# Attention on one core: the projections that run beside the attention steps are cut from pieces of 512 columns into pieces of 256

## The chip, the core and the metric

The kernel is one program on one core of one Trainium2 chip. The core has a matrix engine (TensorE, PE in the profile, with its weight loads listed as PEld), a vector engine (VectorE, DVE), an activation engine (ScalarE, ACT), a general engine (GpSimd, POOL) and a queue that starts most of the DMA transfers (SyncE, SP). Each engine works off its own instruction stream in order; where one needs what another makes, it waits for a semaphore. Matmuls write into PSUM, in banks of 128 partitions by 512 float32 columns.

The metric is the device time of one execution in microseconds (us). Lower is better.

## The reference

A state `x` of 4096 tokens by 256 features passes through four residual layers: attention a, a soft mixture of experts, attention b, and the mixture of experts again with the same weights. Each gets the layer norm of its input.

```python
x = x + attn_a(layernorm(x), Wq, Wk, Wv, Wo, bo, denom_bias)
x = x + ffn(layernorm(x), phi_w, phi_b, expert_w, expert_b)
x = x + attn_b(layernorm(x), q_w, k_w, v_w, o_w)
x = x + ffn(layernorm(x), phi_w, phi_b, expert_w, expert_b)

def attn(x):                     # 16 heads of 16 features, 1 x 4096 x 256
    q, k, v = heads(x @ Wq.T), heads(x @ Wk.T), heads(x @ Wv.T)
    sim = causal(q @ k.T / sqrt(16))
    e = exp(sim - max(sim, -1))
    a = e / (sum(e, -1) + exp(denom_bias))      # the bias in attention a only
    return merge(a @ v) @ Wo.T + bo             # bo in attention a only
```

Everything is float32. In the mixture of experts each token has logits to 64 experts of 32 slots; two softmaxes over them mix tokens into slots and slots back into tokens. Only its edges touch the change.

## The kernel before, in words

**Units and steps.** An attention works in units `(g, b)`: `b` is one of 8 blocks of 512 queries, `g` one of 4 groups of 4 heads. `units` (L339) runs all four groups of block 0, then those of block 1, and so on. A unit has 4(b+1) *steps*, one for each tile of 128 keys up to the diagonal. `steps_b` (L446) yields twice a step: each half makes the scores of two heads in PSUM (`sc`, two matmuls of q and k, L461, and two that subtract the row maxima, `qm`, L466), takes their exponential on ScalarE (L471) and, for a tile on the diagonal, zeroes the upper triangle on GpSimd (`affine_select`, L475). `weigh` (L426) multiplies the exponentials with the values, four heads into one bank `o` (L431); `values_to(1)` keeps it one step behind.

The row maxima must be there before a unit's scores. `steps_a` (L367) makes them ahead, in *pairs*: two matmuls, each into a bank of its own (L380), and two reductions on VectorE (L394, or L388 with the mask where the tile is on the diagonal). How many pairs each step takes is spread evenly by `due` and `wanted` (L551 to L566). `net.bank()` hands out the banks for pairs, projections and transpositions alike, from one pool of three (L329); in the last unit and in the expert layer `net.banks` is a pool of one.

**The order in a step** is written out in the loop at L591 to L616:

```python
want = wanted(n + 1)
maxima_to((done_a[0] + want) // 2)   # about half of the step's pairs
net.beside(2)                        # at most one piece of other work
values_to(1)                         # the o matmuls of the step before
maxima_to(want)                      # the rest of the pairs
```

The prediction calls the first group of pairs A and the last one B. Matmuls and transpositions are kept in the program's order (L67, L70); other instructions may be moved by the scheduler where nothing depends on it.

**Pieces.** `net.beside(k)` (L79) moves a clock on by k, starts what is due on an agenda, and takes one piece from the `urgent` queue, or if that is empty from the `side` queue. `pieces(b)` (L186) lists a block's work for `side`: two normalizations of a token tile (`scale`, on GpSimd at L157, or on ScalarE with `fast`, L152; in attention a the bias is added to `x` at L162), an empty piece, a transposition of two tiles (`turn`, TensorE and a ScalarE copy, L201), an empty piece, the same again for the other two tiles, then two pieces for k and two for q (`part`, L203: 128 output features by the block's 512 tokens, two matmuls accumulating over the 256 input features), and two for v (`values`, L219: two token tiles of 256 features each). That makes 16 pieces. `part` ends in `split` (L165): the projection's leading bits are copied into one half of a buffer by ScalarE (L172), the rest into the other by VectorE (L173), and SP starts the DMAs that lay both out in DRAM (one for k, L175; two for q, L181). There are two such buffers, `hl`, used in turn.

Blocks 0 to 3 of attention a are projected before the first step by `dense` (L234); at `g == 0` of block b = 0 to 3 the loop appends `pieces(b + 4)` (L592). At `g >= 2` of block 3 and later, what is still in `side` is run off before the next unit needs it (L607).

When a unit's values are complete, `epilogue` inverts the sums (6 ticks of the clock later), scales the output (L509, 8 later) and stores it; after the fourth group it fetches the block's output back, and 8 ticks after that two `project` pieces (L530) enter `urgent`: each multiplies two token tiles with `wo` and adds them to `x` (L539). After the second one the block is written to DRAM.

**Attention b's first blocks** are prepared in the expert layer between the attentions. Its last loop goes over 32 token tiles t; from t = 7 it runs one piece a tile, between two halves of the tile's matmuls (L1113). At t = 6 and t = 10 it appends `pieces(0)` and `pieces(1)` with `fast=True` and `values=False`, 14 pieces each (L1126); what is left after the last tile runs off at L1130. The values of these blocks are then made at the start of attention b by `dense_values` (L261).

Of the kernel before, what the change touches and what calls it, by code (L numbers as in the profile page):

```python
# [19 lines left out]
P = 128  # L20
S = 4096
D = 256
NT = S // P
QB = 512
NQB = S // QB
H = 16
HD = 16
# [15 lines left out]
class _Net:  # L43
# [22 lines left out]
    def mm(self, *a, **k):  # L66
        self.tc.keep_in_program_order(self.nc.tensor.matmul(*a, **k))  # L67
# [38 lines left out]
class _Attention:  # L106
# [55 lines left out]
            nc.gpsimd.tensor_tensor(x[:, t, :], x[:, t, :], self.bot, ALU.add)  # L162
        return y

    def split(self, ps, cc, dst, key, part=None):  # L165
        nc = self.net.nc
        two = part is not None
        if not two:
            part = self.hl[self.nhl % 2]
            self.nhl += 1  # L170
        hi, lo = part[:, 0, :], part[:, 1, :]
        nc.scalar.copy(hi.bitcast(F32R), ps)  # L172
        nc.vector.tensor_tensor(lo.bitcast(F32R), ps, hi, ALU.subtract)  # L173
        if key:
            nc.sync.dma_start(  # L175
                dst[ts(cc, 8)].bitcast(F32).rearrange("h e r l t -> (h e) r (l t)"),
                part.rearrange("p l t -> p (l t)").unsqueeze(1).to_broadcast([P, 2, 2 * QB]),
            )
            return
        for r in range(2):  # L180
            (nc.scalar if two and r else nc.sync).dma_start(  # L181
                dst[ts(cc, 8), :, :, r].bitcast(F32).rearrange("h e l t -> (h e) l t"), part
            )


    def pieces(self, b, fast=False, values=True):  # L186
        net, nc = self.net, self.net.nc
        xb, ys = self.xb[b % 2], {}
        idle = lambda: None

        def scale(i):
            if i == 0:
                self.begin(b)
            ys[i] = self.norm(4 * b + i, fast)

        def turn(t2):
            ps = net.bank().rearrange("p (c i t) -> p c i t", c=2, i=2)
            for i in range(2):
                for c in range(2):
                    net.tr(ps[:, c, i, :], ys[2 * t2 + i][:, ts(c, P)])  # L200
            nc.scalar.copy(xb[:, :, ts(t2, 2 * P)], ps.rearrange("p c i t -> p c (i t)"))  # L201

        def part(w, cc, key):  # L203
            ps = net.bank()
            for c in range(2):
                net.mm(ps, w[:, c, ts(cc, P)], xb[:, c, :], start=c == 0, stop=c == 1)
            self.split(ps, cc, (self.kd if key else self.qd)[b], key)

        out = []
        for t2 in range(2):  # L210
            out += [lambda i=i: scale(i) for i in (2 * t2, 2 * t2 + 1)]
            out += [idle, lambda t2=t2: turn(t2), idle]
        for w, key in ((self.wk, True), (self.wq, False)):
            out += [lambda a=(w, cc, key): part(*a) for cc in range(2)]
        if values:
            out += self.dense_values(b)
        return out

    def values(self, b, t2, ps):  # L219
        net, xb = self.net, self.xb[b % 2]  # L220
        ps = ps.rearrange("p (i d) -> p i d", i=2)
        for i in range(2):
            for c in range(2):
                net.mm(
                    ps[:, i, :], xb[:, c, ts(2 * t2 + i, P)], self.wv[:, c, :],
                    start=c == 0, stop=c == 1,
                )
        net.nc.scalar.copy(
            self.vah[:, ds(4 * b + 2 * t2, 2), :, 0:HD],
            ps.rearrange("p i (h e) -> p i h e", e=HD),  # L230
        )
# [32 lines left out]
    def run(self, ready, experts):  # L264

        net, tc, nc = self.net, self.net.tc, self.net.nc
        x, mm = net.x, net.mm
        bo, db = self.bo, self.db
        self.xd = net.xd = net.xds.pop(0)
        with ExitStack() as ctx:  # L270
            pool = lambda n, b, **k: ctx.enter_context(tc.tile_pool(name=f"at_{n}", bufs=b, **k))
            cp = pool("c", 1)
            wo = self.wo
# [10 lines left out]
                out=maskw, in_=maskw, compare_op=ALU.is_ge, fill=NEG,  # L284
# [11 lines left out]
            for p in range(2):  # L296
                f = net.ep.tile([P, QB], F32, name="ot", bufs=3)[:, 0:P]
                nc.gpsimd.memset(f, 0.0)
                for h2 in range(2):
                    for l in range(2):  # L300
                        nc.gpsimd.affine_select(
                            out=f, in_=f, compare_op=ALU.not_equal, fill=1.0,
# [182 lines left out]
            def epilogue(u, ot):  # L485
                g, b = units[u]
                if g == 0:
                    self.ad[b] = net.dram.tile([2 * P, QB], F32, name=f"{self.name}o{b}")
                d16 = net.ep.tile([P, 16], F32, name="d16", bufs=3)
                dd = net.dram.tile([P, 16], F32, name="dd", bufs=3)  # L490
                nc.sync.dma_start(d16, ot[HD:P:32, :].rearrange("j (c s) -> j c s", s=16))
                rb = {}

                def invert():
                    if db is not None:
                        nc.vector.tensor_scalar(d16, d16, edb[:, g : g + 1], None, ALU.add)
                    nc.vector.reciprocal(d16, d16)
                    rb[0] = net.ep.tile([P, QB], F32, name="rb")
                    nc.sync.dma_start(dd, d16)
                    nc.sync.dma_start(  # L500
                        rb[0],
                        dd.rearrange("(j c) s -> j (c s)", j=HG).unsqueeze(1)
                        .to_broadcast([HG, 32, QB]),
                    )
                    net.after(8, divide)

                def divide():
                    on = rb[0]
                    nc.gpsimd.tensor_tensor(on, ot, on, ALU.mult)  # L509
                    for j in range(HG):  # L510
                        nc.sync.dma_start(
                            self.ad[b][ds((HG * g + j) * HD, HD), :], on[ds(32 * j, HD), :]
                        )
                    if g == NG - 1:
                        net.after(4, fetch)

                back = {}

                def fetch():
                    for i2 in range(2):  # L520
                        ao = net.ep.tile([P, 2, 2 * P], F32, name="ao", bufs=2)
                        nc.sync.dma_start(
                            ao, self.ad[b].rearrange("(c p) t -> p c t", p=P)[:, :, ts(i2, 2 * P)]
                        )
                        back[i2] = ao
                    net.after(
                        8, lambda: net.urgent.extend([lambda: project(0), lambda: project(1)])
                    )

                def project(i2):  # L530
                    ps = net.bank().rearrange("p (i d) -> p i d", i=2)
                    for i in range(2):
                        for c in range(2):
                            mm(
                                ps[:, i, :], back[i2][:, c, ts(i, P)], wo[:, c, :],
                                start=c == 0, stop=c == 1,
                            )
                    xs = x[:, ds(4 * b + 2 * i2, 2), :]
                    nc.vector.tensor_tensor(xs, ps, xs, ALU.add)  # L539
                    if i2:  # L540
                        nc.sync.dma_start(self.xd[:, ts(b, 4), :], x[:, ts(b, 4), :])

                net.after(6, invert)
# [46 lines left out]
            n = 0  # L590
# [634 lines left out]
```

## Time and profile before

| | us |
|---|---|
| median of 3 runs | 5162.35 (5161.54 to 5167.37) |
| the profiled execution | 5168.77 |
| its span, first to last instruction | 5167.0 |

The profiled execution has a mean granted TensorE clock of 0.989 of full speed. The span by stage, with the busy time of the engines in it (windows of the trace; a stage ends where the next one's steps begin):

| stage | from, to | length | PE | DVE | ACT | POOL |
|---|---|---|---|---|---|---|
| front | 0, 86.7 | 86.7 | 61.3 | 40.9 | 33.4 | 28.0 |
| attention a, steps | 86.7, 1787.5 | 1700.8 | 1651.4 | 1411.7 | 1101.0 | 172.9 |
| experts, first | 1787.5, 2670.8 | 883.3 | 841.1 | 664.3 | 213.8 | 402.9 |
| attention b, steps | 2670.8, 4367.0 | 1696.2 | 1651.4 | 1405.6 | 1100.7 | 162.8 |
| experts, second | 4367.0, 5167.0 | 800.0 | 780.3 | 624.2 | 181.7 | 391.6 |

Busy time on TensorE comes from modelled ends of pipelined matmuls, so a high share says only that the engine has always something in flight. A float32 matmul appears as two records, of the same shape. In the rows below, a group of instructions shows its source line, engine, operation, output tile and input tiles, shapes and count, then busy time and the mean of one in nanoseconds, then the idle time of the engine just before and what ended it. A timeline's line shows the start, the length in us, the engine, the line, the tiles, how many records it folds together, and in brackets the idle time before it and its cause. Times are counted from the start of the span. L67 is the helper through which every matmul goes, so groups of matmuls are told apart by their tiles.

The pieces that the change touches, by shape, all of them in the span:

| what | line | count | mean ns |
|---|---|---|---|
| k and q parts beside the steps, ScalarE copy 128x512 | L172 | 40 | 583 |
| the same, VectorE subtraction | L173 | 40 | 691 |
| output projections, VectorE addition 128x512 | L539 | 32 | 689 |
| values, ScalarE copy 128x512 (16 of them by `dense_values`) | L228 | 32 | 589 |

### The profile page before, as it was taken

The page shows a single profiled execution, that of the slowest core. Times are in us where ns is not written, and L with a number is a line of the kernel's source. Part 1 is how long each engine was busy: PE and PEld are TensorE (multiplying, and loading weights), DVE is VectorE, ACT ScalarE, POOL GpSimd, SP SyncE. Part 2 cuts the span into 40 slices and gives each one's busy share as a digit, 9 for nine tenths or more (in the row PEclk, how much of TensorE's full clock was granted, in tenths as well). Part 3 has the DMA queues.
Part 4 walks back from the last instruction along what each step waited for, and adds up shares of the span by engine and source line. Part 5 has one row for each costly group of instructions (what it writes and reads, how often), then busy time and mean ns, then how long its engine had stood idle before and what let it go on. Part 6 is the DMA issues. An engine that isn't in the chain of part 4 may idle for free.

```text
span 5167.0 us, 79440 instructions
## 1 busy us (share of the span) xinstructions
PE 4985.5 (96%) x29936; PEld 2669.9 (52%) x29936; DVE 4146.6 (80%) x7800; ACT 2630.7 (51%) x3112; POOL 1158.2 (22%) x1088
## 2 busy tenths in 40 slices
PE   7899999999999999999989999999999999999899
PEld 4444454444455444448854444544444554444588
DVE  5678989898989378777756789888989893887786
ACT  3466676666667721223224666666666677211222
POOL 3211000000000155544411110000000001555453
PEclk9999999999999999999999999999999999999999
DMA  6433222221121013443454342222212210134443
GB/s 254 143 108 125 66 76 65 65 68 58 61 65 56 28 76 106 146 143 120 144 181 143 108 128 68 70 65 69 65 58 64 62 56 32 76 104 149 135 150 110
DMA packets 266449, 499.17 MB, mean 97 GB/s; under 512 B 44976, under 2 KB 110000, under 8 KB 258384
## 3 DMA queue, kind: packets, MB, share of 16 engines
q1 hardware_dynamic: 260832, 485.57, 28.6%
q10 hardware_dynamic: 4896, 7.87, 0.5%
q8 instruction: 235, 3.85, 0.3%
q14 instruction: 150, 1.23, 0.1%
q0 software_dynamic: 336, 0.66, 0.0%
HBM read 336.73 MB, written 156.76 MB: 96 GB/s over the span
## 4 chain that ended last, share of the span: by engine, by line
PE 72%; DVE 13%; POOL 5%; issue 3%; ACT 3%; DMA 2%; SPq 0%; DVEq 0%; POOLq 0%; ACTq 0%
PE o L67 26%; PE bank L67 21%; PE sc L67 16%; DVE mx L394 5%; PE acc L67 4%; PE lg L67 3%; DVE junk L388 3%; POOL e L690 2%; POOL e L698 2%; PE ps L70 2%; ACT e L691 1%; DVE l L677 1%; ACT pb L471 1%; DMA zone<-ld 1%; DMA rb<-dd 0%
## 5 line engine op out<-in xcount | busy, mean ns | idle before, releaser
L471 ACT ACTIVATE pb<-sc 128x1024 f32<-128x1024 f32 (+3 forms) x2304 | 2070.7, 951 | 1132.5 <-PE sc L67 1131.0
L394 DVE TENSOR_REDUCE mx<-bank 128x1 f32<-128x512 f32 x3584 | 2223.0, 682 | 157.5 <-PE bank L67 151.7
L67 PE MATMUL bank<-k,q 64*128 64x512 f32 (+3 forms) x4608 | 1333.9, 451 | 65.0 <-DVE mx L394 26.8
L67 PEld LDWEIGHTS bank<-k,q 64*128 64x128 f32 x4608 | 664.7, 185 | 1177.1 <-DVE mx L394 767.7
L67 PE MATMUL o<-pb,va 128*32 128x512 f32 (+3 forms) x9216 | 1159.7, 574 | 9.1 <-POOL pb L475 7.3
L67 PE MATMUL sc<-q,k 64*128 64x512 f32 (+3 forms) x4608 | 982.5, 389 | 11.3 <-ACT pb L471 10.9
L67 PE MATMUL sc<-qm,one 64*128 64x512 f32 (+3 forms) x4608 | 945.2, 376 | 0.0
L388 DVE CUSTOM_DVE_ANT_0 junk<-bank,maskw 128x128 bf16<-128x128 f32 (+3 forms) x1024 | 502.6, 491 | 253.5 <-PE bank L67 145.8
L475 POOL TENSOR_SCALAR_AFFINE_SELECT pb<-pb 128x256 f32<-128x256 f32 x512 | 205.0, 407 | 2170.0 <-ACT pb L471 2162.7
L67 PEld LDWEIGHTS sc<-q,k 64*128 64x128 f32 x4608 | 507.7, 187 | 129.7 <-issue 50.6
L67 PEld LDWEIGHTS sc<-qm,one 64*128 64x128 f32 x4608 | 524.1, 187 | 68.5
L67 PE MATMUL acc<-e,x 128*128 128x512 f32 x1008 | 464.4, 604 | 22.4 <-POOL e L698 17.8
L691 ACT ACTIVATE e<-e 128x1024 f32<-128x1024 f32 x126 | 133.1, 1057 | 690.2 <-POOL e L690 690.2
L67 PE MATMUL lg<-zone,xnT 128*128 128x512 f32 x1008 | 455.4, 593 | 8.3 <-DVE l L677 7.1
L67 PE MATMUL o<-ys,lT 128*128 128x256 f32 x2048 | 459.5, 381 | 0.0
L67 PEld LDWEIGHTS o<-ys,lT 128*128 128x128 f32 x2048 | 385.6, 191 | 56.5 <-issue 6.6
L67 PEld LDWEIGHTS o<-pb,va 128*32 128x32 f32 x9216 | 183.6, 108 | 319.6 <-issue 286.3
L889 POOL TENSOR_TENSOR e<-l,mc 128x1024 f32<-128x1024 f32 x120 | 281.4, 2365 | 283.3 <-DMA l<-ld 180.5
L67 PEld LDWEIGHTS acc<-e,x 128*128 128x128 f32 x1008 | 189.2, 192 | 264.3 <-issue 211.4
L698 POOL TENSOR_TENSOR e<-e,s 128x1024 f32<-128x1024 f32 x126 | 240.9, 1912 | 366.5 <-DVE s L697 345.0
L67 PEld LDWEIGHTS lg<-zone,xnT 128*128 128x128 f32 x1008 | 189.3, 190 | 245.0 <-issue 213.9
L696 DVE TENSOR_REDUCE s<-e 128x32 f32<-128x1024 f32 x126 | 153.6, 1219 | 158.3 <-ACT e L691 158.1
(136 smaller groups left out, 3229.7 us busy)
## 6 DMA issues: line engine op xcount, KB each, us to landing
k<-ak SPq DMA_DIRECT2D x144, 512.0 KB
k<-bk SPq DMA_DIRECT2D x144, 512.0 KB
ld<-l SPq DMA_DIRECT2D x126, 512.0 KB
l<-ld SPq DMA_DIRECT2D x60, 1024.0 KB
w<-in_L_ffn_expert_w_dram SPq DMA_DIRECT2D x26, 1024.0 KB
q<-aq SPq DMA_DIRECT2D x32, 512.0 KB
rb<-dd SPq DMA_DIRECT2D x64, 256.0 KB
q<-bq SPq DMA_DIRECT2D x32, 512.0 KB
```

The costliest lines, as they stand in the source:

```text
L67: self.tc.keep_in_program_order(self.nc.tensor.matmul(*a, **k))
L70: self.tc.keep_in_program_order(self.nc.tensor.transpose(o, i, self.ident))
L388: nc.vector.tensor_tensor_reduce(out=junk[:, 0:w], in0=scs[h2][:, 0:w], in1=maskw[:, QB - w : QB], scale=1.0, scalar=-3e38, op0=ALU.add, o ...
L394: nc.vector.tensor_reduce(m, scs[h2], AX.X, ALU.max)
L471: nc.scalar.activation(pb[:, :, off:QB], sc[:, :, off:QB], AF.Exp)
L475: nc.gpsimd.affine_select(out=d, in_=d, compare_op=ALU.is_ge, fill=0.0, base=0, pattern=[[0, 2], [1, P]], channel_multiplier=-1,)
L677: net.nc.vector.tensor_tensor(l, lg, self.phb[:, ds(h * (E // 2) + n * 512, 512)], ALU.add)
L690: nc.gpsimd.tensor_tensor(e3, l3, _bc(m.unsqueeze(2), [P, ne, SLOT]), ALU.subtract)
L691: nc.scalar.activation(e, e, AF.Exp)
L696: nc.vector.tensor_reduce(s, e3, AX.X, ALU.add)
L698: nc.gpsimd.tensor_tensor(e3, e3, _bc(s.unsqueeze(2), [P, ne, SLOT]), ALU.mult)
L889: nc.gpsimd.tensor_tensor(e[:, ns, :], l, _bc(cms[t].unsqueeze(1), [P, NH, SLOT]), ALU.subtract)
```

## The change

Each k, q, v and output projection that runs as a piece is cut in two, and each half is a piece of its own, so it is taken in a step (or token tile) of its own. The dense front of attention a and `dense_values` stay as they are.

- `part` takes a half `n`: two matmuls of 256 columns into half a bank.
- `split` works on the half's columns of the same `hl` buffer, moves to the other buffer with each first half, and starts its DMAs after the second half alone.
- The values of `pieces` come from a new method `value`, one token tile at a time.
- `project` works on one token tile; four of them enter `urgent`, and the DMA to DRAM follows the fourth.

A list of `pieces` so grows from 16 to 22 (14 to 18 without values).

```diff
-    def split(self, ps, cc, dst, key, part=None):
+    def split(self, ps, cc, dst, key, part=None, n=None):
         nc = self.net.nc
         two = part is not None
         if not two:
+            self.nhl += n == 0
             part = self.hl[self.nhl % 2]
-            self.nhl += 1
-        hi, lo = part[:, 0, :], part[:, 1, :]
+        cut = part if n is None else part[:, :, ts(n, QB // 2)]
+        hi, lo = cut[:, 0, :], cut[:, 1, :]
         nc.scalar.copy(hi.bitcast(F32R), ps)
         nc.vector.tensor_tensor(lo.bitcast(F32R), ps, hi, ALU.subtract)
+        if n == 0:
+            return
         if key:
...
-        def part(w, cc, key):
-            ps = net.bank()
+        def part(w, cc, key, n):
+            ps = net.bank()[:, 0 : QB // 2]
             for c in range(2):
-                net.mm(ps, w[:, c, ts(cc, P)], xb[:, c, :], start=c == 0, stop=c == 1)
-            self.split(ps, cc, (self.kd if key else self.qd)[b], key)
+                net.mm(
+                    ps, w[:, c, ts(cc, P)], xb[:, c, ts(n, QB // 2)],
+                    start=c == 0, stop=c == 1,
+                )
+            self.split(ps, cc, (self.kd if key else self.qd)[b], key, n=n)
...
         for w, key in ((self.wk, True), (self.wq, False)):
-            out += [lambda a=(w, cc, key): part(*a) for cc in range(2)]
+            out += [lambda a=(w, cc, key, n): part(*a) for cc in range(2) for n in range(2)]
         if values:
-            out += self.dense_values(b)
+            out += [lambda t=t: self.value(b, t) for t in range(4)]
         return out
+
+    def value(self, b, t):
+        net, xb = self.net, self.xb[b % 2]
+        ps = net.bank()[:, 0:D]
+        for c in range(2):
+            net.mm(ps, xb[:, c, ts(t, P)], self.wv[:, c, :], start=c == 0, stop=c == 1)
+        net.nc.scalar.copy(
+            self.vah[:, 4 * b + t, :, 0:HD], ps.rearrange("p (h e) -> p h e", e=HD)
+        )
...
-                        8, lambda: net.urgent.extend([lambda: project(0), lambda: project(1)])
+                        8, lambda: net.urgent.extend([lambda i=i: project(i) for i in range(4)])
...
-                def project(i2):
-                    ps = net.bank().rearrange("p (i d) -> p i d", i=2)
-                    for i in range(2):
-                        for c in range(2):
-                            mm(
-                                ps[:, i, :], back[i2][:, c, ts(i, P)], wo[:, c, :],
-                                start=c == 0, stop=c == 1,
-                            )
-                    xs = x[:, ds(4 * b + 2 * i2, 2), :]
+                def project(i):
+                    ps = net.bank()[:, 0:D]
+                    for c in range(2):
+                        mm(
+                            ps, back[i // 2][:, c, ts(i % 2, P)], wo[:, c, :],
+                            start=c == 0, stop=c == 1,
+                        )
+                    xs = x[:, 4 * b + i, :]
                     nc.vector.tensor_tensor(xs, ps, xs, ALU.add)
-                    if i2:
+                    if i == 3:
                         nc.sync.dma_start(self.xd[:, ts(b, 4), :], x[:, ts(b, 4), :])
```

## The prediction

> **What bounds the kernel now.** I read the page's busy row and its chain first, then the timelines of one bare step and one step that carries a piece, then the groups by shape.
>
> ```profile
> PE 4985.5 (96%) x29936; PEld 2669.9 (52%) x29936; DVE 4146.6 (80%) x7800; ACT 2630.7 (51%) x3112; POOL 1158.2 (22%) x1088
> PE 72%; DVE 13%; POOL 5%; issue 3%; ACT 3%; DMA 2%; SPq 0%; DVEq 0%; POOLq 0%; ACTq 0%
> PE o L67 26%; PE bank L67 21%; PE sc L67 16%; DVE mx L394 5%; PE acc L67 4%; PE lg L67 3%; DVE junk L388 3%; POOL e L690 2%; POOL e L698 2%; PE ps L70 2%; ACT e L691 1%; DVE l L677 1%; ACT pb L471 1%; DMA zone<-ld 1%; DMA rb<-dd 0%
> ```
>
> Busy PE alone proves little, but the chain also runs 72% over PE. The stage to be changed shows why. These are TensorE's timeline (start, length, tile) and VectorE's, around one projection in attention a, query block b=4:
>
> ```profile
> 896.77 0.50 PE L67 MATMUL bank<-k,q 64*128 64x512 f32 x2
> ...
> 898.03 0.52 PE L67 MATMUL bank<-k,q 64*128 64x512 f32 x2
> 898.48 1.06 PE L67 MATMUL o<-pb,va 128*32 128x512 f32 x8
> 899.48 0.50 PE L67 MATMUL bank<-k,q 64*128 64x512 f32 x2
> ...
> 900.74 0.51 PE L67 MATMUL bank<-k,q 64*128 64x512 f32 x2
> 901.36 1.99 PE L67 MATMUL bank<-zone,ao 128*128 128x256 f32 x8
> 903.28 1.06 PE L67 MATMUL o<-pb,va 128*32 128x512 f32 x8
> 904.28 0.50 PE L67 MATMUL bank<-k,q 64*128 64x512 f32 x2
> ```
>
> ```profile
> 900.01 2.48 DVE L394 TENSOR_REDUCE mx<-bank 128x1 f32<-128x512 f32 x4 [0.22 <-PE bank L67]
> 903.46 0.69 DVE L539 TENSOR_TENSOR x<-bank,x 128x512 f32<-128x512 f32 x1 [0.96 <-PE bank L67]
> ```
>
> The bare step, 896.77 to 899.48, takes 2.71 us: eight score matmuls, a maxima pair A, the eight o matmuls, a maxima pair B, without a hole. The step with the piece, 899.48 to 904.28, takes 4.80, and VectorE waits 0.96 us for TensorE in it. So a step with a piece is TensorE's: a piece pays its matmuls, plus the seams at its two ends.
>
> **What a piece costs, and what half a piece will.** A project, k/q or value piece is 1.72 us of matmuls (8 records of 256 columns start every 0.2155, or 4 of 512 every 0.429). The projection step is 4.80 - 2.71 = 2.09 longer, so the seams are 2.09 - 1.72 = 0.37. They can be seen: from A to the piece is 0.62 us (900.74 to 901.36) against 0.45 from A to o in the bare step, as the piece takes the third bank, which waits for the reduction of B before it (+0.17); its first two starts lie 0.32 apart in place of 0.2155 (+0.10); from its last start, 902.97, to o are 0.31 (+0.09). None of the three shrinks with columns. A k piece agrees: the step at 466.98 takes 4.78. So half a piece is 0.86 + 0.36 = 1.22, and two are 2.44 in place of 2.08: **each added piece costs 0.36**. The copy and subtraction end under the o matmuls as now.
>
> **How many are added.** Groups by shape, as engine, shape, count | busy, mean ns | idle:
>
> ```profile
> L172 ACT CAST zone<-bank 128x512 fp32r<-128x512 f32 x40 | 23.3, 583 | 65.2 <-PE bank L67 63.4 <-issue 1.9
> L173 DVE TENSOR_TENSOR zone<-bank,zone 128x512 fp32r<-128x512 f32 x40 | 27.6, 691 | 44.5 <-ACT zone L172 42.9 <-DMA q<-bq 0.6 <-DMA bk<-zone 0.3
> L964 DVE TENSOR_TENSOR x<-o,xl 128x256 f32<-128x256 f32 x64 | 27.2, 424 | 114.3 <-PE o L67 113.9
> ```
>
> 40 k/q parts become 80, the 32 projections (L539) 64, and 16 of the 32 value pieces become 32: 88 more. Taking one piece a step off the queue as beside() does puts 76 of them in attention steps (38 in each attention: 14 in b=0-1, 8 each in b=2 and b=3, 8 in b=4-7), 8 in the first expert part's weighing of tokens and its drain, 4 (the last block's projections) in expert steps.
>
> Two rules of the Trainium skill bear here. The row is a 512-column subtraction of 691 ns against 424 for 128x256 (L964), so two halves take 848, +157. "VectorE: DVE Perf Modes", section "The TRN2 errata", says that each instruction pays a fixed bubble and to tile at 512 elements or more; it speaks against this change. By that rule, with VectorE as the bound, 72 split evacuations x 0.157 = 11 us. By the timeline VectorE stands idle for 0.96 in such a step, so I take 0 for this, and charge the seams. "TensorE: Matmul & The Clock Gate", section "Wait — 56ns, not 53.3ns?", gives a matmul a fixed 2.5 ns; the 160 more records of the 40 split parts would then cost 0.4 us, and the change nothing. The row's starts, 0.2155 for 2 x 256 columns, agree inside a run of matmuls, but the rule has no seam, and 76 x 0.36 = 27.4 us is what the seams make. I take the row: **+27.4**, from 76 x 0.20 = 15 (if the bank wait vanishes) to 76 x 0.50 = 38 (if a bank comes free late as well, an estimate with another 0.14).
>
> **Shifts.** (1) Block 4's pieces no longer fit in the 16 steps of b=0; 6 slip into b=1, and block 5's k, q and values go from b=1 g=0-2 to g=2-3. That moves a GpSimd stall, seen on its timeline:
>
> ```profile
> 177.86 1.29 POOL L509 TENSOR_TENSOR rb<-ot,rb 128x512 f32<-128x512 f32 x1 [14.19 <-DMA k<-ak]
> 179.13 2.42 POOL L157 TENSOR_SCALAR zone<-x,mv,rstd 128x256 f32<-128x256 f32 x2
> 181.52 1.40 POOL L162 TENSOR_TENSOR x<-x,bot 128x256 f32<-128x256 f32 x2
> 182.87 1.48 POOL L475 TENSOR_SCALAR_AFFINE_SELECT pb<-pb 128x256 f32<-128x256 f32 x4
> ```
>
> The diagonal's select stands in GpSimd's queue behind the scaling of block 5, which runs as soon as turn 5 frees its buffer; o waits 4.0 us for it, and the step takes 8.30 (5.68 in attention b) against 2.59 before it. Afterwards turn 5 comes in g=1, two steps ahead of the diagonal, and the stall should go: between 0 and 5.7 + 3.1 = 8.8 us. I take **-6**, as scaling may meet another select. What is late next there is VectorE, with six reductions a step.
>
> (2) The six-reduction steps that receive block 5's halves (3.6-4.0 us) hide little: TensorE waits about 0.42 in them, before the last matmul of B (the record at 249.60 of TensorE's timeline), and the half stands ahead of that, between A and o. I charge it in full.
>
> (3) After each block's last projection ScalarE loads two tables (2 x 1.28) and normalizes x for the expert part. q and v pieces hid under that at b=1-3; fewer matmuls stand there now: 0 to 6 us, I take **+3**, half.
>
> (4) The drain. In the weighing stage one piece runs a token tile, tiles 7 to 31: 25 turns for 28 pieces before, 36 after. What is left runs alone, with one bank:
>
> ```profile
> 2610.61 1.88 PE L67 MATMUL bank<-zone 128*128 128x512 f32 x4
> 2613.90 1.98 PE L67 MATMUL bank<-zone 128*128 128x512 f32 x4 [1.40 <-DVE zone L173]
> 2617.32 3.71 PE L67 MATMUL bank<-zone 128*128 128x512 f32 x12 [1.45 <-DVE zone L173]
> ```
>
> Each 512 part is a chain of matmul, copy, subtraction, 3.43 us; three of them end, with the next piece starting at 2619.36, after 8.75. Afterwards a transposition (4 x 0.11, 0.16 of tail, the 0.59 copy, 0.1: 1.3) and 8 halves are left. A half is 3.43 - 0.86 (matmuls) - 0.2 (copy; 0.38 by L471's 128x256 row) - 0.27 (subtraction) = 2.1; seven of them, the last 2.04 - 0.86 = 1.2, and the 1.3 make 17.2. The weighing loses a transposition and a part, 0.44 + 1.72 = 2.2, which it paid in full (the part at 2605.44 has no seam). Net 17.2 - 8.75 - 2.2 = **+6.2**; 4 to 10.
>
> The split shares its buffer and issues its DMAs once, after the second half, so SP's queue holds no more issues; between a buffer's DMA and its next writing lie two half steps (7.8 us) in place of one (4.8): no wait. The four late projections cost about 0.1 each in expert steps: +0.4.
>
> **Sum.** 27.4 - 6 + 3 + 6.2 + 0.4 = **+31 us**. It is made against the profiled execution, 5168.77 (its span 5167.0 and 1.8 around it), which lies 6.4 over the median of the runs, 5162.35. On the median: **5193**, +0.6%. About 0.2% (10 us) is what a measurement of this kernel tells from no change.
>
> **Rivals.**
> - *Seams vanish* (13%): half pieces fit into waits (PE waits 3.9 us on VectorE's L388 in 161-283) and cost matmuls only. Then -6 + 3 + 6.2 = +3: 5165. For it: early steps of 3-6 us. Against: no hole in the steps of b=3-7.
> - *Relief, faster* (9%): halves fit where TensorE waits for a bank anyway. Block 5's 12 halves in g=2-3 of b=1 then cost nothing and give back 6 x 2.08 = 12.5 an attention, 25 in all; the seams of the other 64 lose their bank wait (x 0.20 = 12.8); the GpSimd stall goes whole (-8.8), the tables cost nothing, drain and late projections 6.6: -14, 5148. It decides if TensorE's wait after B in a six-reduction step is over 0.86 us, the half's matmuls; I read 0.42.
> - *Late banks* (15%): evacuations come late for the next A; 0.6 a piece, 46 us, drain 10, stall stays, tables 6: +62, 5224.
> - *The order of unpinned work shifts* (a table load or scaling lands badly): within the range.
>
> The base case has 63%, with 5172 to 5216 from its low ends (15 - 8.8 + 0 + 4 = +10) and high ends (38 + 0 + 6 + 10 = +54). Range 5164 to 5216, to take in the vanished seams. Faster 0.09; same 0.14; slower 0.77.
>
> **What would show it.** Half steps of 3.9 us in b=3 with 4 records of 256 columns and 0.6 us from A to them; projection steps at b=4-7 four, of about 3.9; no 8.30 step at b=1; a drain of some 17 us before the value pieces of attention b; 80 casts of about 380 ns at L172. I am wrong if half steps take 3.6 or less, or if six-reduction steps stay at 4.0 with a half in them.

## The result, and the profile after

The changed kernel takes 5182.72 us in the median of 7 runs (5177.10 to 5185.74) against 5163.63 for the kernel before beside it (5161.54 to 5175.49, 7 runs). The ratio is 1.0031, 95% interval 1.0021 to 1.0042: slower by 16 us, between 11 and 22. The forecast was 31 us slower, twice as much.

The profiled execution took 5185.74 us, its span 5183.8, at a mean clock of 0.987 (0.989 before). Its page, the busy row and the chain:

```profile
PE 5001.4 (96%) x30096; PEld 2699.2 (52%) x30096; DVE 4167.1 (80%) x7872; ACT 2638.8 (51%) x3168; POOL 1158.3 (22%) x1088
PE 75%; DVE 13%; POOL 4%; issue 3%; ACT 3%; DMA 2%; DVEq 0%; SPq 0%; POOLq 0%; ACTq 0%
```

There are 160 more matmul records than before and the chain runs a little more over TensorE; that tells nothing of where 17 us went. The starts of the steps do. The table sets two pairs of traces of the two kernels (the first traces, and one more of each taken later) against the prediction's own terms, in us:

| stretch | predicted | first pair | second pair |
|---|---|---|---|
| blocks 0 and 1, both attentions | 28 x 0.36 - 6 = +4 | -4.1 | -0.2 |
| blocks 2 and 3 | 32 x 0.36 = +11.6 | +8.0 | +7.0 |
| blocks 4 to 7 | 16 x 0.36 = +5.8 | -6.0 | -4.2 |
| ScalarE's tables, over all blocks | +3 | (in the rows above) | |
| from attention a's last step to attention b's first | -2.2 + 8.45 + 0.4 = +6.6 | +17.9 | +15.9 |
| front and second experts | 0 | +1.0 | -0.8 |
| sum | +31 | +16.8 | +17.7 |

So the attention steps, 60 of whose 76 added pieces lie in blocks 0 to 3, cost almost nothing together (-2.1 and +2.6), and the expert layer that ends in the drain holds the whole loss. The half steps themselves came out as forecast. A block's output projection is now four pieces of one token tile, called quarter projections below; each is half of an old piece. TensorE's timeline of the changed kernel, around two of them in block 5's steps:

```profile
902.32 0.52 PE L67 MATMUL bank<-k,q 64*128 64x512 f32 x2
902.94 1.13 PE L67 MATMUL bank<-zone,ao 128*128 128x256 f32 x4
904.00 1.07 PE L67 MATMUL o<-pb,va 128*32 128x512 f32 x8
904.99 0.50 PE L67 MATMUL bank<-k,q 64*128 64x512 f32 x2
...
906.26 0.51 PE L67 MATMUL bank<-k,q 64*128 64x512 f32 x2
906.87 1.13 PE L67 MATMUL bank<-zone,ao 128*128 128x256 f32 x4
```

From one piece to the next are 3.93 us (902.94 to 906.87); 0.62 lie between A and the piece, as they do with a whole one. 3.93 - 2.70, the bare step, is 1.23 for half a piece; the prediction had 1.22. The smaller evacuations (the copies were forecast at about 380 ns), in the groups by shape (count | busy, mean ns | idle):

```profile
L174 DVE TENSOR_TENSOR zone<-bank,zone 128x256 fp32r<-128x256 f32 x80 | 33.8, 423 | 45.3 <-ACT zone L173 45.3
L173 ACT CAST zone<-bank 128x256 fp32r<-128x256 f32 x80 | 29.7, 372 | 43.6 <-PE bank L67 42.1
```

What paid for the seams is seen after each block's last projection. ScalarE's timeline there, first of the kernel before (projections of block 5):

```profile
1184.82 1.94 ACT L471 ACTIVATE pb<-sc 128x1024 f32<-128x1024 f32 x2 [2.89 <-PE sc L67]
1186.78 1.28 ACT L99 ACT_TABLE_LOAD   x1
1188.07 0.30 ACT L99 ACTIVATE rstd<-mv,eps 128x4 f32<-128x4 f32 x1
1188.39 1.28 ACT L471 ACT_TABLE_LOAD   x1
1189.68 1.94 ACT L471 ACTIVATE pb<-sc 128x1024 f32<-128x1024 f32 x2
```

and of the changed kernel:

```profile
1187.16 1.94 ACT L487 ACTIVATE pb<-sc 128x1024 f32<-128x1024 f32 x2 [1.99 <-PE sc L67]
1189.12 1.28 ACT L99 ACT_TABLE_LOAD   x1
1190.41 0.30 ACT L99 ACTIVATE rstd<-mv,eps 128x4 f32<-128x4 f32 x1
1191.09 1.28 ACT L487 ACT_TABLE_LOAD   x1 [0.38 <-PE sc L67]
1192.38 1.94 ACT L487 ACTIVATE pb<-sc 128x1024 f32<-128x1024 f32 x2
```

VectorE's timeline up to the variances, before (both tiles together) and changed (the last tile):

```profile
1182.93 0.69 DVE L539 TENSOR_TENSOR x<-bank,x 128x512 f32<-128x512 f32 x1 [0.83 <-PE bank L67]
1183.66 0.75 DVE L94 BATCH_NORM_STATS2 st<-x 128x6 f32<-128x256 f32 x2
1184.33 1.27 DVE L394 TENSOR_REDUCE mx<-bank 128x1 f32<-128x512 f32 x2
1185.52 0.24 DVE L95 BATCH_NORM_AGGREGATE mv<-st 128x2 f32<-128x6 f32 x2
```

```profile
1189.21 0.42 DVE L554 TENSOR_TENSOR x<-bank,x 128x256 f32<-128x256 f32 x1
1189.67 0.43 DVE L94 BATCH_NORM_STATS2 st<-x 128x6 f32<-128x256 f32 x1
1190.14 0.18 DVE L95 BATCH_NORM_AGGREGATE mv<-st 128x2 f32<-128x6 f32 x1
```

and TensorE's next wait for ScalarE, before and changed:

```profile
1190.76 0.50 PE L67 MATMUL sc<-q,k 64*128 64x512 f32 x2 [0.82 <-ACT pb L471]
1193.46 0.50 PE L67 MATMUL sc<-q,k 64*128 64x512 f32 x2 [0.17 <-ACT pb L487]
```

Before, the step with the last projection has its exponentials done at 1181.9 and ScalarE idles for 2.89 us while TensorE works at the piece; the loads come only after the next step's exponentials, in a bare step that leaves no such hole, and TensorE then waits 0.82 us for ScalarE. In the changed kernel the loads stand in the last piece's own step, right behind its exponentials (1189.12, while the quarter's matmuls end at 1189.1), and TensorE waits 0.17.

The drain before attention b, TensorE's timeline of the changed kernel:

```profile
2613.67 0.60 PE L70 MATMUL bank<-ident,zone 128*128 128x128 f32 x4
2614.95 1.13 PE L67 MATMUL bank<-zone 128*128 128x256 f32 x4 [0.68 <-ACT zone L204]
2617.29 1.13 PE L67 MATMUL bank<-zone 128*128 128x256 f32 x4 [1.22 <-DVE zone L174]
2619.37 1.13 PE L67 MATMUL bank<-zone 128*128 128x256 f32 x4 [0.95 <-DVE zone L174]
2621.42 1.65 PE L67 MATMUL bank<-zone 128*128 128x256 f32 x4 [0.92 <-DVE zone L174]
2623.99 2.07 PE L67 MATMUL bank<-zone 128*128 128x256 f32 x4 [0.92 <-DVE zone L174]
2627.03 2.08 PE L67 MATMUL bank<-zone 128*128 128x256 f32 x4 [0.96 <-DVE zone L174]
```

and windows over it (stretch, its length, busy time of the five engines, then the granted clock, the DMA share and GB/s):

```profile
2620.00:2630.00 10.00, 6.30 (x15) 3.27 (x13) 1.70 (x4) 1.49 (x4) 0.00 (x0) 0.59 0.87 311
2640.00:2650.00 10.00, 7.91 (x39) 5.17 (x37) 2.96 (x15) 4.42 (x8) 0.00 (x0) 1.00 1.01 367
```

The first halves follow each other every 2.05 to 2.08 us, the chain of matmul, copy and subtraction that the prediction had at 2.1. From 2621 on the same four records take 2.07 in place of 1.13 and the chain 3.0: the clock is at a half. From the transposition to the first value piece, at 2634.89, it is 21.2 us (23.1 in the second trace), where 17.2 were forecast and the kernel before took 8.75 at full clock.

The additions of the token tiles (`x<-o,xl` on VectorE, L964 before, L979 in the changed kernel) divide this stage's excess. Up to the 17th tile, which runs ahead of the first k piece, the changed kernel takes 5.6 and 2.8 us more than before, in the first and the second pair. From there to the 32nd and last it takes 142.2 in both, against 144.3: the -2.2 of the forecast. From that to TensorE's next maxima pair, behind the first value piece, it takes 24.6 and 25.4, against 10.2: +14.4 and +15.3. The first of the three is not the cost of half pieces: a kernel with whole pieces in this layer, shown below, has 2.7 of it in one trace and 0.3 in another.

### The profile page after: what moved, and what is told of

Its sections match the earlier page's. It is cut to its first block, busy times and chain, and to the rows that moved or that the text cites. A ratio compares the mean times of both kernels' runs of the same rounds, so it can differ in the third digit from the quotient of the medians.

```text
span 5183.8 us, 79909 instructions
## 1 busy us (share of the span) xinstructions
PE 5001.4 (96%) x30096; PEld 2699.2 (52%) x30096; DVE 4167.1 (80%) x7872; ACT 2638.8 (51%) x3168; POOL 1158.3 (22%) x1088
## 4 chain that ended last, share of the span: by engine, by line
PE 75%; DVE 13%; POOL 4%; issue 3%; ACT 3%; DMA 2%; DVEq 0%; SPq 0%; POOLq 0%; ACTq 0%
PE o L67 27%; PE bank L67 21%; PE sc L67 16%; DVE mx L410 6%; PE acc L67 5%; PE lg L67 4%; DVE junk L404 3%; POOL e L705 2%; PE ps L70 2%; POOL e L713 1%; ACT e L706 1%; ACT pb L487 1%; DVE l L692 1%; DVE lT L962 0%; DMA d<-ot 0%
## 5 line engine op out<-in xcount | busy, mean ns | idle before, releaser
L67 PE MATMUL bank<-k,q 64*128 64x512 f32 (+3 forms) x4608 | 1320.5, 451 | 65.0 <-DVE mx L410 30.1
```

## The experiments

Each run stands beside the kernel before on the same chip. "Blocks 4 to 7" is the time of their steps in one attention, 1150.4 and 1150.3 us in the first trace of before (attention a and b), 1149.2 and 1150.0 in the second. The times of runs of one kernel spread by 10 to 20 us; in the traces, part of that is where the clock stands at a half in blocks 0 and 1 of an attention (190 us each). Blocks 4 to 7 repeat to about a microsecond, so theories are told apart there.

**The parts apart.** First the projections alone:

```diff
-  net.urgent.extend([lambda: project(0), lambda: project(1)])
+  net.urgent.extend([lambda i=i: project(i) for i in range(4)])
   # with the changed kernel's project; k, q and values as before
```

> Only the output projections are split: four project pieces of one token tile a block in place of two; k, q and values as before. 28 pieces more stand in the attention steps, 4 in expert steps. Theory (each piece more costs its seams, 0.36, but the fourth projection falls under the load of ScalarE's tables, which stalled TensorE after the last projection, and so that stall shrinks by 0.7 to 2.7 a block): 28 x 0.36 = +10, +1 in expert steps, -14 x 1.2 = -17: some -6 us on before, between -12 and 0. Rival (only the seams change, the table stall stays): +11 us. Rival (seams cost nothing in a step that VectorE or ScalarE holds): 0 to +1 for the pieces and -17 for the stall: -16 us.

Measured: ratio 0.9991 (0.9983 to 1.0000), -5 us, as the theory had it, though hardly clear of no change. Blocks 4 to 7 take 1147.8 and 1148.1. Their eight added pieces, at 0.36, would add 2.9; they come out 2.6 and 2.2 lower, so some 5 us an attention went.

Then k, q and values alone, `project` as before:

> The complement: k, q and values in halves as in the changed kernel, the output projections in two pieces as before. Theory: 48 pieces more in the attention steps, 48 x 0.36 = +17, less the GpSimd stall of block 1 (-6), plus the drain before attention b (+14 with the half clock in it): +25 us, between +18 and +30. If the effects of the two parts add, it is the measured +16 to +19 less what the projections alone give. Rival (half pieces of k, q and v cost nothing beside the steps): +8 us.

Measured: 1.0059 (1.0046 to 1.0071), +30 us, at the upper end. The stage before attention b is 14.7 us longer than before (897.9 against 883.2), the attention steps 4.2 and 5.5. The sum of the two parts is +26, against +16 for both together; with intervals of 4 to 7 us to either side, that may be scatter.

**Is the table load the stall?** The square root of the variances by Newton steps on VectorE:

```diff
-  nc.scalar.activation(r, self.mv[:, lo:hi, 1], AF.Sqrt, bias=self.eps)
+  v = self.mv[:, lo:hi, 1]
+  h = self.shift[:, lo:hi]
+  nc.vector.tensor_scalar(r, v, 1.0, 0.5, ALU.add, ALU.mult)
   nc.vector.reciprocal(r, r)
+  for _ in range(4):
+      nc.vector.scalar_tensor_tensor(h, r, -0.5, r, ALU.mult, ALU.mult)
+      nc.vector.tensor_tensor(h, h, v, ALU.mult)
+      nc.vector.scalar_tensor_tensor(r, h, 1.5, r, ALU.add, ALU.mult)
```

> The kernel before, but the reciprocal root of the variances is made by four Newton steps on VectorE in place of ScalarE's square root, so that no table is loaded between the exponentials of an attention. Theory (the tables' load stalls TensorE by 1.8 us after each block's last projection, up to 3 in the early blocks): 14 blocks x 1.8 to 3, less about 0.5 of VectorE in each: -20 us, between -35 and -10. Rival (the stall is ScalarE's normalization of x or is caught up in the following steps): 0, or some us slower for the added VectorE work.

A miss: 1.0027 (1.0016 to 1.0038), 14 us slower, and blocks 4 to 7 at 1150.7 and 1150.9, no better. VectorE's timeline shows why this run doesn't answer the question:

```profile
1196.51 0.16 DVE L104 SCALAR_TENSOR_TENSOR shift<-rstd 128x4 f32<-128x4 f32 x1
1196.70 0.16 DVE L105 TENSOR_TENSOR shift<-shift,mv 128x4 f32<-128x4 f32 x1
1196.90 0.16 DVE L106 SCALAR_TENSOR_TENSOR rstd<-shift,rstd 128x4 f32<-128x4 f32 x1
```

Four columns cost 0.19 us from start to start, so twelve such instructions take 2.3 us of an engine that has 0.2 us of idle time in a bare step, and TensorE then waits for a reduction (0.33 us at 1198.11). One stall was traded for another. Most of the 14 us lie elsewhere: the stage before attention b, where roots are taken too, is 11.6 us longer. A cleaner test leaves the root out and adds nothing:

```diff
-  nc.scalar.activation(r, self.mv[:, lo:hi, 1], AF.Sqrt, bias=self.eps)
+  nc.scalar.activation(r, self.mv[:, lo:hi, 1], AF.Identity, bias=self.eps)
```

> The kernel before with the square root of the variances left out (ScalarE adds the constant and takes no root, so it loads no other table between the exponentials); everything else is issued as before. Theory (the two table loads after a block's last projection stall TensorE by some 1.8 us): the steps of blocks 4 to 7 take 1.8 x 4 = 7 us less in each attention, 1143 in place of 1150. Rival (ScalarE's normalization of x sets that stall, or it is caught up): 1149 or more.

> The projections in four pieces and nothing else split, and the square root left out as in the run beside it. Theory (the split gains only by putting the fourth projection under the table loads): without them it loses its seams, 2 x 0.36 a block, 4 blocks: blocks 4 to 7 take 2.9 us more in each attention than in the run beside it with two projection pieces. Rival (the gain comes from elsewhere, as from statistics made a tile at a time): still 2 us or more less than it.

Each of these two kernels ran once, and its trace is what is read here. Without the root, blocks 4 to 7 take 1144.7 and 1144.3: 5.7 and 6.0 less than with the loads, 1.4 to 1.5 a block. ScalarE's timeline has the hole closed:

```profile
1182.17 1.94 ACT L471 ACTIVATE pb<-sc 128x1024 f32<-128x1024 f32 x2 [2.88 <-PE sc L67]
1184.00 0.30 ACT L99 ACTIVATE rstd<-mv,eps 128x4 f32<-128x4 f32 x1
1184.91 1.94 ACT L471 ACTIVATE pb<-sc 128x1024 f32<-128x1024 f32 x2 [0.61 <-PE sc L67]
```

With quarter projections and no root they take 1147.2 and 1146.5: 2.5 and 2.2 more than with the old two pieces and no root, where eight seams at 0.36 make 2.9. With the root, the same split gained 2.6 and 2.2. So the seams are still paid, to within the microsecond that such sums repeat to, and the gain hangs on the table loads: of the 5.7 to 6.0 us that they cost in four blocks, the split leaves 0.6 and 1.6 (1147.8 - 1147.2, 1148.1 - 1146.5).

**Is it the place or the size that costs?** The halves of the changed kernel, two to a piece, so at the steps of the kernel before:

```diff
-  out += [lambda a=(w, cc, key, n): part(*a) for cc in range(2) for n in range(2)]
+  out += [lambda a=(w, cc, key): [part(*a, n) for n in range(2)] for cc in range(2)]
   # the values and the projections likewise, two token tiles to a piece
```

> The halves of the changed kernel, but two of them taken in one step as one piece: the same small matmuls, copies, additions and the same number of them, at the steps of the kernel before. Theory (an added piece pays 0.36 for its own place between A and o, and not for being half as wide): in a clean step two halves cost 2.09 to 2.3 and not 2.46, so the attention steps come out within 5 us of before, and only the drain is left: +12 us, between +5 and +16. Rival (small instructions pay by themselves, VectorE's 0.157 a pair and the fixed costs of more matmuls): in a clean step 2.46 or more, and the kernel at +20 us or above.

For the steps the theory holds. TensorE's timeline of that kernel, projections of block 5:

```profile
1177.74 0.51 PE L67 MATMUL bank<-k,q 64*128 64x512 f32 x2
1178.35 1.99 PE L67 MATMUL bank<-zone,ao 128*128 128x256 f32 x8
1180.27 1.06 PE L67 MATMUL o<-pb,va 128*32 128x512 f32 x8
```

Eight records follow the same 0.61 us after A as one piece of two tiles did, and the step takes 4.79 (4.82 before in the same step); a k step takes 4.78, as before. Two small copies and subtractions in place of one large pair cost nothing there. Blocks 4 to 7 even fall to 1146.0 in both attentions, since the added tiles' statistics come sooner here too and no place was added. The total was misjudged: 1.0041 (1.0026 to 1.0056), +21 us. The stage before attention b is 24.6 us longer. There the pieces share one bank, and the second half of each pair waits 0.92 us for the first one's subtraction, in the middle of a token tile as well: by the additions of the token tiles, 12.1 us come between the 17th and the last, 7.7 in the drain and behind it, and 4.8 ahead of the first k piece.

**The drain.** The changed kernel with whole pieces in the expert layer, in two separate sets of runs:

```diff
+  if fast:
+      out += [lambda a=(w, cc, key): whole(*a) for cc in range(2)]   # 512 columns
+  else:
       out += [lambda a=(w, cc, key, n): part(*a) for cc in range(2) for n in range(2)]
```

> The changed kernel, but the pieces of attention b's first two blocks, which run in the first expert layer, are whole again (512 columns, 14 a block). Theory (the loss of the change sits in the drain at the end of the expert layer: eight chains of matmul, copy, subtraction in place of two and a bit, and a half clock that comes with them): about 14 us less than the changed kernel, so +2 us on before, within -3 to +6; the row of the granted clock shows no half clock between the last token tile and attention b. Rival (the seams in the attention steps are the loss, and the drain is within the scatter): it stays at +12 to +19.

> The changed kernel once more, for a second trace and beside the next run on the same chip. Theory: the half clock of some 17 us lies in the drain again, and the stage from the end of attention a's steps to the first of attention b is 16 to 18 us longer than before, with attention steps within 5 us of before: +17 us, between +12 and +22. Rival (the half clock in the drain was chance): the stage 10 to 13 us longer.

> The changed kernel with whole pieces in the expert layer, once more: its first trace put all of the change's loss into the drain, while the times of its first runs left it at +7 to +15. Theory (the drain is the loss): the stage before attention b as long as before within 2 us, and the runs some 12 us under those of the changed kernel beside it. Rival (its attention steps lose as well, and the first trace was a lucky one): attention steps 4 us or more over before in each attention, and less than 8 us under the changed kernel.

The stage before attention b: 883.5 and 887.5 us with whole pieces, 901.1 and 899.0 in the changed kernel, 883.2 and 883.1 in the two traces of before. No half clock stands in the drain with whole pieces, while the two traces of the changed kernel have 17 and 20 us of it there. So the drain holds the loss of that stage, 14 us on average; of the 4.3 us that are left in the second trace with whole pieces, 2.7 come ahead of the first k piece. For the whole kernel the expectation of +2 missed, as did that of 12 us under the changed kernel (8.5 were measured beside it): ratios 1.0021 (1.0013 to 1.0030) and 1.0019 (1.0010 to 1.0028), +10 us, against +16 and +17 (1.0033, 1.0022 to 1.0045) for the changed kernel. In the traces the difference is in blocks 0 and 1, where the pieces are the same: 387.4 and 390.5 us in both attentions together, 383.5 and 383.0 in the changed kernel. The granted clock there differs from trace to trace (0.88 to 0.91 with whole pieces, 0.87 to 0.95 in the changed kernel). Whether a half clock in the drain leaves less of it for the following blocks, or this is scatter, stays open.

Then the drain of the changed kernel through two banks, the second one idle at that point:

```diff
+  turns = 0
   while net.side:
+      if turns % 2:
+          net.bank = lambda: two.tile([P, 512], F32, name="bank2")
       net.beside(3)
+      net.__dict__.pop("bank", None)
+      turns += 1
```

> The changed kernel, but in the drain before attention b the pieces take a second bank in turn (one that is idle there), so that a half's matmuls run beside the copy and subtraction of the half before. Theory (the drain is a chain through one bank, and TensorE's idle time in it lets the clock fall to a half): the drain from the transposition to the first value piece falls from 21.2 to about 11 us, the clock stays at full, and the kernel gains 10 us on the changed one: +6 us on before, between 0 and +10. Rival (the half clock comes from the DMAs that run there at 310 GB/s, or at a set time, not from the idle time): the half clock stays and the gain is 4 us at most.

A part of it came: the drain took 14.5 us (2606.56 to 2621.06; 11 were expected), the stage 889.6, 11.5 less than in the changed kernel's first trace; the runs lie at 1.0028 (1.0016 to 1.0039), too near the changed kernel to tell them apart. ScalarE's timeline names the next thing that was late:

```profile
2611.88 0.70 ACT L173 CAST zone<-bank 128x256 fp32r<-128x256 f32 x2
2616.38 0.65 ACT L173 CAST zone<-bank 128x256 fp32r<-128x256 f32 x2 [3.79 <-DMA bk<-zone]
2620.17 0.37 ACT L173 CAST zone<-bank 128x256 fp32r<-128x256 f32 x1 [3.15 <-DMA bk<-zone]
```

The copies of q wait until the DMA of k has read the buffer that they write; there are two such buffers. And a half clock came behind that wait (0.66 over 2616 to 2621), not before it, though the DMAs moved more in the five microseconds ahead (407 GB/s at clock 1.00, then 311). The drain of the kernel before kept clock 1.00 as well with 333 and 397 GB/s (2610 to 2615, 2615 to 2620). So the DMAs alone don't bring the half clock; that the idle time does is argued, not shown.

**A version that beats both.** Before's pieces, whole and in their places; only `project` in blocks 0 to 6 handles its two tiles one after the other, and the drain takes two banks:

```diff
   def project(i2):
+      if b < NQB - 1:
+          for i in range(2):
+              ps = net.bank()[:, 0:D]
+              for c in range(2):
+                  mm(ps, back[i2][:, c, ts(i, P)], wo[:, c, :], start=c == 0, stop=c == 1)
+              xs = x[:, 4 * b + 2 * i2 + i, :]
+              nc.vector.tensor_tensor(xs, ps, xs, ALU.add)
+          ...
```

> The kernel before with two edits: a project piece of blocks 0 to 6 adds its two token tiles one at a time, each from a bank of its own, in the step it has now (so no place is added); and the drain before attention b takes two banks in turn. k, q and values whole. Theory (an added piece pays for its place and not for its size; the finer addition lets the variances, and with them the table load, come in the last projection's own step): blocks 4 to 7 at 1146 in each attention as in the run with pairs, blocks 1 to 3 some 1 us less each, the drain 2 us less: -12 us on before, between -18 and -5. Rival (the pairs' gain needs k, q and values in halves too): -2 us, no difference that the runs can tell.

Measured: 5149.95 us median of 5 (5139.91 to 5154.88), ratio 0.9968 (0.9955 to 0.9980), 16 us faster than before. The trace is that of the fastest of the five runs; in it, blocks 4 to 7 take 1146.4 and 1145.4, and the stage before attention b 877.6, 5.6 less than before, 3.4 of it in the drain. ScalarE's timeline after the projections of block 5:

```profile
1174.96 1.94 ACT L471 ACTIVATE pb<-sc 128x1024 f32<-128x1024 f32 x2 [2.87 <-PE sc L67]
1176.91 1.28 ACT L99 ACT_TABLE_LOAD   x1
1179.00 0.30 ACT L99 ACTIVATE rstd<-mv,eps 128x4 f32<-128x4 f32 x1 [0.81 <-DVE mv L95]
1179.75 1.28 ACT L471 ACT_TABLE_LOAD   x1 [0.45 <-PE sc L67]
```

The first load sits in the hole of the last projection's step, where the root behind it even waits for its data (0.81); the second load follows in the next step. In the drain, TensorE's timeline has three whole k and q parts and the first value piece in one run, with no wait:

```profile
2601.30 7.04 PE L67 MATMUL bank<-zone 128*128 128x512 f32 x20
```

**The scatter.**

> The kernel before once more, against itself: what two sets of runs of one kernel differ by, and a second trace for the half clock in blocks 0 and 1. Theory: a ratio within 0.1% of one; the clock at full in the drain before attention b; the stages within 2 us of the first trace but for blocks 0 and 1 of each attention, where the half clock falls by chance, within 8 us. Rival (chips or hours differ by more): a ratio off by 0.15% or more.

The kernel before against itself: 1.0001 (0.9992 to 1.0009). The stage before attention b repeats to 0.1 us, blocks 0 and 1 of both attentions to 4.4 (387.6 and 383.2).

## Why the prediction came out as it did

The direction and the price of a piece were right. The size was half of what was forecast, and that it came so near is in part luck: the tables' term was too high by some 12 us in blocks 4 to 7 alone, the drain's too low by 6 to 7, and the two errors cancel in part.

- **0.36 for each added piece: right.** Half steps take 3.93 (forecast 3.9), the seam is the same 0.62 between A and the piece, and the pairs show that it belongs to the place: two halves in one place cost what a whole piece does. The rule of the Trainium skill that small VectorE tiles pay, in "VectorE: DVE Perf Modes", section "The TRN2 errata" (155 ns more for two halves by the rows, 157 forecast), did not decide anything there, as the prediction chose.
- **Six-reduction steps hide little: right.** In attention a's block 1, g=2, kt=4, the step went from 4.07 to 5.38 (first score matmul to first score matmul), +1.31 for a half; over the twelve such steps with halves it is 1.12 on average. With that, the rival "relief" falls as it was put: no half fitted into a wait.
- **The GpSimd stall: it went, but -6 was not safe.** The step that the prediction has at 8.30 us (5.68 in attention b) takes 3.94 with a half piece in it. But in the second trace of the kernel before it takes 4.07 in attention a: TensorE waits 0.95 us there for GpSimd, and 3.96 in the first trace. And a wait came in three steps earlier, at kt=2, where a half piece stands now: the step takes 7.8 and 8.3 us in attention a (the two traces of the changed kernel) and 8.8 and 8.7 in attention b, against 5.4 and 6.8, and 4.5 and 4.5, before. TensorE waits there, 1.48 us in attention a and 2.81 in attention b of the first trace, for a half's subtraction (L174), which stands in VectorE's queue behind work on a unit's sums (L512, L513) that waits for its DMA. It is what the rival "late banks" describes, in one step of each attention.
- **(3), the tables: the step that failed, in its sign.** It read: "fewer matmuls stand there now: 0 to 6 us, I take +3, half." It asked what piece lies beside the loads and not when the root can run. The root stands behind the first load in ScalarE's queue and needs the variances of the last tile. With a piece of two tiles, VectorE adds both (0.69), takes statistics of both (0.75), and aggregates only after the next two reductions, from 1185.52, when the hole has ended at 1184.82. A tile at a time, the addition, the statistics and the aggregation are done 1.3 us after the piece in place of 3.0. That was worth about 5 us an attention in blocks 4 to 7 (2.6 and 2.2 gained with the root, 2.5 and 2.2 lost without it). For blocks 1 to 3 it wasn't isolated. The prediction's last rival had named a table load that shifts, but as one that lands badly.
- **(4), the drain: the right chain, too small a sum.** 2.05 to 2.08 a half were measured for 2.1; at that pace some 17 us would have come out (an estimate), as forecast. The half clock added 4.0 in the drain of the first trace and 1.7 in the first value piece (eight records every 0.427 in place of 0.2155). Weighing and drain together are +12.3 and +13.2, for the +6.2 of the forecast. The rest of the stage's excess, 5.6 and 2.8, arises ahead of the first k piece and is not the drain's; its cause stays open.
- **Blocks 0 and 1** gave 4 to 8 us less than forecast, in a stretch where the kernel before differs from itself by 4.

## What to carry to other kernels

Work laid beside a bound engine pays for each place in which it is put, so cut it only where the smaller size lets something start sooner; and then cut inside the place, as the projections of the last version do, which take the gain and add no seam. Before a piece is moved or cut, ask of each instruction that hangs on its end (here a table load two instructions further on) in which hole of its engine it will fall. A serial remainder through one buffer multiplies with the number of pieces, and here its short waits came together with a half clock of the matrix engine.

## What the runs showed of the hardware

- The clock halves without a long pause. In the drain TensorE never stood idle for more than 1.22 us at once, yet after one to three halves (0.86 us of matmuls in each 2.05) the clock went to a half and stayed there for 17 and 20 us in the two traces of the changed kernel, for 17 in that of k, q and v alone, and for 14 in that of the pairs. Before's drain, with 1.72 us of matmuls in each 3.4 and waits of 1.40 and 1.45, kept full clock. The Trainium skill, "TensorE: Matmul & The Clock Gate", section "A second HAM failure mode: psum-queue depth-cycling", describes such short waits between groups of matmuls, as PSUM banks are cycled, that let the clock go up and down; this trace agrees. The share of time filled with matmuls, 42% here and 50% there, may be what decides, but two points don't make a threshold. The moment also has a part of chance: with whole pieces, the four 512-column records at 2632.27 of the second trace took 3.35 us, at half clock, and the same four in the first trace (2631.59) 1.98.
- A table load is 1.28 us and the next instruction starts 0.01 us after it (1186.78 to 1188.07).
- A VectorE instruction on 128x4 costs 0.19 us from start to start. A dozen of them took as much from the steps as the two loads that they replaced: 1150.7 and 1150.9 us in blocks 4 to 7, against 1150.4 and 1150.3.
